# Values visits followed directly by scores, and transposes ahead of the first inputs, in a two-layer graph attention kernel

## The chip, the cores and the metric

The kernel runs on one core of one Trainium2 chip. The metric is the device time of one execution in microseconds, lower is better; the figure for a kernel is the median of its runs. All data are float32.

## The reference

The input is x with 64 graphs of 256 nodes and 512 features, and one adjacency matrix of 256 x 256 that all graphs share. Each of two layers normalises x, applies relu and adds its result to x. The first layer is masked attention of 8 heads with 64 features each, the second a graph attention with one score per node and side.

```python
    h = jnp.maximum(_layernorm(x, axis=-1), 0.0)
    x = x + _L0_gnn_ref(h, adj, L0_gnn_Wq, ..., L0_gnn_bo)
    h = jnp.maximum(_layernorm(x, axis=-1), 0.0)
    x = x + _L1_gnn_ref(h, L1_gnn_W, L1_gnn_a, L1_gnn_beta, adj)
# layer 0, of h: q, k, v = h @ Wq + bq, h @ Wk + bk, h @ Wv + bv, in heads
    scores = jnp.einsum('bqhd,bkhd->bhqk', q, k) / jnp.sqrt(jnp.float32(HD))
    scores = scores + (1.0 - adj)[None, None, :, :] * -1000000000.0
    attn = jax.nn.softmax(scores, axis=-1)
    out = jnp.einsum('bhqk,bkhd->bqhd', attn, v).reshape(b, n, d)
    return out @ Wo + bo
# layer 1, of h: h = h @ W, s1 = h @ a1, s2 = h @ a2
    e = jax.nn.leaky_relu(s1[:, :, None] + s2[:, None, :], negative_slope=ALPHA)
    e = e * mask[None, :, :]
    att = jax.nn.softmax(e, axis=2)
    h_prime = jnp.einsum('bij,bjf->bif', att, h)
    return jax.nn.elu(h_prime + beta * h)
```

## The kernel before

The graphs are worked on in 32 pairs. A pair's two graphs, with the two halves of their 512 features, form a matrix of 2 x 2 blocks, and every dense product (q and k, v, the output projection, the second layer's W) is computed in the Strassen manner with seven block products instead of eight. A `Unit` is one such product. `u.p(i)` issues product i: four matmuls on q's and k's side each (`UnitQK`, line 321) or eight matmuls (`UnitV`, `UnitO`, `UnitW`, line 354) of 128 x 128 by 256. Products are issued in the order 1, 4, 6, 2, 7, 5, 3. Products 2 and 3 add into the PSUM banks of products 1 and 5. `products` also calls what empties the banks: `put11` after product 2, `put2` after product 5, `put12` after product 3. So the bank of product 5, `b`, is written by PE, read by VectorE (DVE) in `put2` (lines 339, 455 or 562), added to by product 3, and read again in `put12`.

The sums of blocks that the seven products need are made by `combine_31`, `combine_2` and `combine_4`. For the output projection the two of `combine_31` are `o_blocks`, on GpSimd (POOL, line 427), and `combine_2` (line 273) on DVE subtracts from the second of them; product 6 of `UnitO` reads that.

Beside the dense products there are visits of the attention:

- `scores(b, q)`, line 385: for graph b and half q of the heads, 16 matmuls of 64-row tiles (two heads side by side in the array) into four banks; ScalarE (ACT, line 389) takes the exponential of each into a tile pt; POOL multiplies it by the mask (line 390) and adds its two halves into pp (line 392). A callback may be placed between these.
- `values(b, q)`: 32 matmuls of 32-column tiles (line 403) and 8 for the row sums (line 412); DVE takes the reciprocal (1.7 us), adds to acc and writes the tile oT (lines 414 to 417). It returns a closure that adds the reciprocals to acc on POOL (line 418); the closure is called at once or handed to the next scores as a callback.

The pt pool has four buffers, as many as one visit of scores fills, so each scores follows the values of the scores ahead of it. PSUM has eight banks, taken and given back in the order of the program.

For the second layer `gat_scores`, `gat_exp`, `divide` and `gat_t` make the attention matrix: DVE forms e (lines 488, 490), ACT takes the exponential, `divide` scales it on DVE (line 502), and PE transposes it (line 511, eight transposes for two graphs). `gat_z` multiplies (line 525), and `UnitW` ends the layer and stores.

The instruction order is written out by hand. `tc.manual_schedule` keeps each engine's instructions in the order of the program: for PE throughout, for DVE, ACT and POOL from `first` on. Only in most of `start` (all but the normalising and transposing of the first pair) a planner orders DVE, ACT and POOL by its own estimate. SyncE (SP) issues every DMA.

`start` handles pair 0's projections, `first` and `second` fill the pipeline, `round(p)` for p from 2 to 30 is the steady state, `last` and `end` drain it. One round runs the second layer of pair p - 2 (`UnitW`), the output projection of pair p - 1 (`UnitO`), the attention of pair p (graphs g0 and g1, four visits of scores and four of values) and the projections of pair p + 1 (`UnitQK` twice: ua and ub; `UnitV`: uv). In a round `x_t` transposes the next inputs on PE (line 300), `x_scales` and `y_scales` turn statistics into scales partly on POOL (lines 227 to 229), `y_normal` normalises on ACT (line 472), `y_sums` forms the node scores on DVE (line 478), and `residuals` loads x again and adds the bias on POOL (line 435).

Of the kernel before, what the change touches and what calls it, by code (L numbers as in the profile page):

```python
# [16 lines left out]
P = 128  # L17
# [6 lines left out]
def kernel(ctx: ExitStack, tc: tile.TileContext, x, adj, wq, bq, wk, bk, wv, bv, wo, bo, w, a, beta, out):  # L24
# [560 lines left out]
    def x_scales(p):  # L585
        SCALE["x", p] = scales(f"x{p}", 1)
# [8 lines left out]
    def y_stats_0(p):  # L595
        y_stats(p, 2 * NT, 0, 2 * p, 0)
# [5 lines left out]
    def y_stats_2(p):  # L602
        y_stats(p, 2 * NT, 0, 2 * p, 1)
# [25 lines left out]


    def start():
        with tc.manual_schedule(engines={ENG.DVE, ENG.Activation, ENG.Pool}):
            for g in range(2):
                for t in range(NT):
                    stats(f"x0{g}", NT, t, 0, XT[g, t])
                rstd, mr = scales(f"x0{g}", 1)
                nmr = minus(mr, f"x0{g}")
                for t in range(NT):
                    nc.scalar.activation(XT[g, t], XT[g, t], AF.Identity, bias=nmr[:, t:t + 1],
                                         scale=rstd[:, t:t + 1])  # L640
            x_t(0)
        combine_24(A["h", 0])
        load(1)
        ua, ub, uv = UnitQK(0, 0), UnitQK(0, 1), UnitV(0)
        products(ua, 1, 4, 6, 2, 7, 5)
        ub.p(1)
        products(ua, 3)
        products(ub, 4, 6, 2, 7, 5)
        masks()
        products(ub, 3)  # L650
        scores(0, 0)
        products(uv, 1, 4, 6, 2, 7, 5)
        wo_blocks = project_b()
        products(uv, 3)
        return wo_blocks

    def first():
        for i in range(2 * NT):
            x_stats(1, i)
        x_scales(1)  # L660
        add = values(0, 0)
        scores(0, 1, {1: add})
        x_normals(1, *range(2 * NT))
        x_t(1)
        load(2)
        s = A["h", 1]
        ua, ub, uv = UnitQK(1, 0), UnitQK(1, 1), UnitV(1)
        ua.p(1)
        combine_24(s)
        products(ua, 4, 6)  # L670
        prods = project_a()
        prods(0)
        products(ua, 2, 7)
        add = values(0, 1)
        prods(1)
        scores(1, 0, {1: add})
        products(ua, 5)
        ub.p(1)
        prods(2)
        products(ub, 4)  # L680
        products(ua, 3)
        products(ub, 6, 2)
        prods(3)
        add = values(1, 0)
        scores(1, 1, {1: add})
        products(ub, 7, 5)
        uv.p(1)
        products(ub, 3)
        prods(4)
        products(uv, 4)  # L690
        for i in range(2 * NT):
            x_stats(2, i)
        values(1, 1)()
        o_blocks(0)
        x_scales(2)
        products(uv, 6)
        combine_2(A["o", 0])
        products(uv, 2)
        x_normals(2, *range(2 * NT))
        products(uv, 7)  # L700
        combine_4(A["o", 0])
        products(uv, 5)
        residuals(0)
        prods(5)
        return uv

    def second(uv):
        p = 1
        scores(2, 0)
        products(uv, 3)  # L710
        uo = UnitO(0)
        products(uo, 1, 4, 6, 2)
        x_t(2)
        load(3)
        products(uo, 7)
        combine_2(A["h", 2])
        y_stats_0(0)
        products(uo, 5)
        add = values(2, 0)
        y_stats_1(0)  # L720
        combine_4(A["h", 2])
        ua, ub, uv = UnitQK(2, 0), UnitQK(2, 1), UnitV(2)
        products(uo, 3)
        y_stats_2(0)
        scores(2, 1, {1: lambda: (add(), y_scales(0))})
        ua.p(1)
        products(ua, 4)
        y_normal(0, 1)
        products(ua, 6, 2)
        y_normal(0, 0)  # L730
        products(ua, 7)
        y_sums(0, 1, 0, 1)
        add = values(2, 1)
        scores(3, 0, {1: add})
        products(ua, 5)
        ub.p(1)
        y_sums(0, 0, 0)
        products(ub, 4)
        products(ua, 3)
        products(ub, 6, 2)  # L740
        y_sums(0, 0, 1)
        add = values(3, 0)
        scores(3, 1, {1: add})
        gat_scores(1)
        gat_scores(0)
        products(ub, 7)
        gat_exp(1)
        gat_exp(0)
        products(ub, 5)
        uv.p(1)  # L750
        products(ub, 3)
        divide(0)
        products(uv, 4)
        gat_t(1)
        gat_t(0)
        values(3, 1)()
        products(uv, 6, 2)
        residuals(1)
        products(uv, 7, 5)
        gat_z(0)  # L760
        products(uv, 3)
        combine_24(A["z", 0])


    def round(p):
        g0, g1 = 2 * p, 2 * p + 1
        scores(g0, 0)
        uw = UnitW(p - 2)
        uw.p(1)
        x_stats(p + 1, 0)  # L770
        x_stats(p + 1, 1)
        uw.p(4)
        x_stats(p + 1, 2)
        x_stats(p + 1, 3)
        products(uw, 6, 2, 7, 5)
        uw.finish(0, 0, nc.gpsimd)
        x_scales(p + 1)
        o_blocks(p - 1)
        add = values(g0, 0)
        scores(g0, 1, {1: add})  # L780
        uw.p(3)
        combine_2(A["o", p - 1])
        x_normals(p + 1, 0, 1)
        uo = UnitO(p - 1)
        uo.p(1)
        uw.finish(1, 1, nc.vector)
        uw.put12()
        uw.finish(1, 0, nc.vector)
        x_normals(p + 1, 2, 3)
        uo.p(4)  # L790
        combine_4(A["o", p - 1])
        uo.p(6)
        uw.finish(0, 1, nc.vector)
        products(uo, 2)
        x_t(p + 1)
        if p + 2 < NP:
            load(p + 2)
        uo.p(7)
        combine_2(A["h", p + 1])
        y_stats_0(p - 1)  # L800
        products(uo, 5)
        add = values(g0, 1)
        y_stats_1(p - 1)
        combine_4(A["h", p + 1])
        products(uo, 3)
        y_stats_2(p - 1)
        scores(g1, 0, {1: lambda: (add(), y_scales(p - 1))})
        ua, ub = UnitQK(p + 1, 0), UnitQK(p + 1, 1)
        products(ua, 1, 4)
        y_normal(p - 1, 1)  # L810
        products(ua, 6)
        y_sums(p - 1, 1, 0, 1)
        products(ua, 2)
        y_normal(p - 1, 0)
        products(ua, 7, 5)
        y_sums(p - 1, 0, 0)
        add = values(g1, 0)
        scores(g1, 1, {1: add})
        products(ua, 3)
        y_sums(p - 1, 0, 1)  # L820
        products(ub, 1, 4, 6)
        gat_scores(g1 - 2)
        products(ub, 2)
        gat_exp(g1 - 2)
        gat_scores(g0 - 2)
        gat_exp(g0 - 2)
        products(ub, 7)
        divide(p - 1)
        products(ub, 5)
        values(g1, 1)()  # L830
        uv = UnitV(p + 1)
        uv.p(1)
        gat_t(g1 - 2)
        gat_t(g0 - 2)
        products(ub, 3)
        products(uv, 4, 6, 2)
        residuals(p)
        if p == NP - 2:
            o_blocks(p, "xt")
        products(uv, 7, 5)  # L840
        if p == NP - 2:
            combine_24(A["o", p])
        gat_z(p - 1)
        products(uv, 3)
        combine_24(A["z", p - 1])

    def last():
        p = NP - 1
        g0, g1 = 2 * p, 2 * p + 1
        scores(g0, 0)  # L850
        uo = UnitO(p - 1)
        products(uo, 1, 4, 6, 2)
        y_stats_0(p - 1)
        products(uo, 7, 5)
        add = values(g0, 0)
        y_stats_1(p - 1)
        products(uo, 3)
        y_stats_2(p - 1)
        scores(g0, 1, {0: lambda: y_scales(p - 1), 1: add})
        uw = UnitW(p - 2)  # L860
        products(uw, 1, 4)
        y_normal(p - 1, 1)
        products(uw, 6)
        y_sums(p - 1, 1, 0, 1)
        products(uw, 2)
        y_normal(p - 1, 0)
        products(uw, 7)
        add = values(g0, 1)
        y_sums(p - 1, 0, 0, 1)
        scores(g1, 0, {1: add})  # L870
        gat_scores(g1 - 2)
        gat_exp(g1 - 2)
        uw.p(5)
        gat_scores(g0 - 2)
        gat_exp(g0 - 2)
        uw.put2()
        uw.finish(0, 0, nc.gpsimd)
        divide(p - 1)
        uw.finish(1, 1, nc.vector)
        products(uw, 3)  # L880
        uw.finish(1, 0, nc.vector)
        add = values(g1, 0)
        scores(g1, 1, {1: add})
        uw.finish(0, 1, nc.vector)
        residuals(p)
        gat_t(g1 - 2)
        gat_t(g0 - 2)
        gat_z(p - 1)
        values(g1, 1)()
        o_blocks(p)  # L890
# [238 lines left out]
```

## Time and profile before

| what | us |
|---|---|
| median of 3 runs | 2918.84 |
| lowest and highest run | 2918.67, 2920.66 |
| the profiled execution | 2920.39 |
| its span from first to last instruction | 2918.5 |
| one steady round (start to start of one visit) | 88.77 |
| POOL pt<-pt,maskT, mean of one | 1.432 |
| POOL pp<-pt, mean of one | 0.827 |
| DVE reciprocal, mean of one | 1.743 |

The profiled execution took 1.9 us more than its span, and 1.6 us more than the median of the runs. In the profile, PE stands for TensorE's matmuls, PEld for its weight loads, which run beside them. A timeline line gives the start, the duration, the engine, the line, the operation with output and inputs, the tile shape, the count, and in brackets the idle time ahead of it with what ended it. The duration of a group of matmuls contains the way through the array, so the cost of a group is read from its start to the next group's start. TensorE's granted clock was 0.992 in the mean; it was full from 16.9 us on, but for short stretches near 68, 92 and in the last 110 us.

### The profile page before, as it was taken

How to read it: one execution, taken by the hardware profiler on the slowest of the kernel's cores; microseconds unless marked ns; L12 is line 12 of the kernel's file. 1: busy time of each engine (PE TensorE's matmuls, PEld its weight loads, DVE VectorE, ACT ScalarE, POOL GpSimd, SP SyncE). 2: the span in 40 equal slices, each digit the busy share in tenths (PEclk: the TensorE clock that was granted, in tenths of full speed). 3: DMA queues.
4: the chain of work that ended last, by engine and by line, in shares of the span. 5: the costliest groups of instructions: out<-in, count | busy, mean ns of one | idle time of the engine just before them, and what ended most of it. 6: DMA issues, size and time to landing. Idle time of an engine off the chain costs nothing.

```text
span 2918.5 us, 46465 instructions
## 1 busy us (share of the span) xinstructions
PE 2870.4 (98%) x18078; PEld 2340.9 (80%) x18078; DVE 2072.1 (71%) x3652; ACT 1043.2 (36%) x2116; POOL 1623.0 (56%) x1588
## 2 busy tenths in 40 slices
PE   8999999999999999999999999999999999999987
PEld 6778888888888888888888888888888888888865
DVE  5657866677767677766778676777666777667765
ACT  2233433333433333333334333334333333333332
POOL 2555655555655556655556555566555565555662
PEclk9999999999999999999999999999999999999998
DMA  5001111001111001110011110011110111100100
GB/s 149 25 11 34 44 44 44 19 26 44 44 44 44 15 30 44 44 44 28 24 37 44 44 44 15 30 44 44 44 43 13 32 44 44 44 23 22 30 30 30
DMA packets 96463, 110.00 MB, mean 38 GB/s; under 512 B 8560, under 2 KB 79472, under 8 KB 96240
## 3 DMA queue, kind: packets, MB, share of 16 engines
q1 hardware_dynamic: 96240, 106.99, 12.0%
q8 instruction: 145, 2.38, 0.3%
q14 instruction: 78, 0.64, 0.1%
HBM read 73.41 MB, written 33.55 MB: 37 GB/s over the span
## 4 chain that ended last, share of the span: by engine, by line
PE 93%; DVE 2%; POOL 2%; issue 2%; ACT 0%; DMA 0%; SPq 0%; POOLq 0%; DVEq 0%; ACTq 0%
PE qk_p L321 26%; PE o_p L354 13%; PE w_p L354 13%; PE v_p L354 13%; PE av L403 8%; PE sc L385 8%; PE pz L525 8%; PE sm L412 2%; PE tr L300 2%; PE at L511 1%; POOL pt L390 1%; POOL pp L392 1%; PE pe L154 0%; DVE pr L478 0%; DVE e L490 0%
## 5 line engine op out<-in xcount | busy, mean ns | idle before, releaser
L390 POOL TENSOR_TENSOR pt<-pt,maskT 128x512 f32<-128x512 f32 x512 | 733.3, 1432 | 772.8 <-ACT pt L389 772.8
L392 POOL TENSOR_TENSOR pp<-pt 128x256 f32<-128x256 f32 x512 | 423.4, 827 | 39.8
L389 ACT ACTIVATE pt<-sc 128x512 f32<-128x512 f32 x512 | 264.4, 603 | 427.4 <-PE sc L385 427.3
L478 DVE SCALAR_TENSOR_TENSOR pr<-h,war 128x512 f32<-128x512 f32 x256 | 298.9, 1211 | 59.2 <-ACT h L472 59.2
L385 PE MATMUL sc<-qk 64*128 64x256 f32 x2048 | 256.4, 390 | 0.0
L403 PE MATMUL av<-pt,v 128*32 128x256 f32 x4096 | 252.4, 383 | 3.0 <-POOL pt L390 3.0
L418 POOL TENSOR_TENSOR acc<-acc,rec 128x256 f32<-128x256 f32 x128 | 109.7, 857 | 253.5 <-DVE acc L415 250.3
L385 PEld LDWEIGHTS sc<-qk 64*128 64x128 f32 x2048 | 187.8, 187 | 65.0 <-issue 20.6
L414 DVE RECIPROCAL rec<-sm 128x256 f32<-128x256 f32 x128 | 223.0, 1743 | 13.9 <-PE sm L412 13.9
L525 PE MATMUL pz<-eT,h 128*128 128x256 f32 x1024 | 229.2, 383 | 3.1 <-ACT eT L512 3.1
L525 PEld LDWEIGHTS pz<-eT,h 128*128 128x128 f32 x1024 | 196.5, 192 | 30.6 <-ACT eT L512 3.6
L403 PEld LDWEIGHTS av<-pt,v 128*32 128x32 f32 x4096 | 130.8, 110 | 105.1 <-issue 40.6
L321 PE MATMUL qk_p<-s_h,wq_t 128*128 128x256 f32 x768 | 198.5, 381 | 0.9 <-DVE s_h L273 0.9
L321 PE MATMUL qk_p<-s_h,wk_t 128*128 128x256 f32 x768 | 197.4, 380 | 0.0
L354 PE MATMUL o_p<-wo_t,s_o 128*128 128x256 f32 x768 | 178.5, 382 | 0.0
L354 PE MATMUL w_p<-w_t,s_z 128*128 128x256 f32 x768 | 177.5, 381 | 0.0
L354 PE MATMUL v_p<-wv_t,s_h 128*128 128x256 f32 x768 | 176.4, 379 | 0.0
L532 DVE TENSOR_TENSOR s_z<-pz,z 128x512 f32<-128x512 f32 x64 | 44.3, 691 | 182.2 <-ACT z L528 182.2
L528 ACT COPY z<-pz 128x512 f32<-128x512 f32 x128 | 74.9, 585 | 254.3 <-PE pz L525 254.3
L354 PEld LDWEIGHTS o_p<-wo_t,s_o 128*128 128x128 f32 x768 | 141.3, 190 | 27.2 <-issue 10.5
L321 PEld LDWEIGHTS qk_p<-s_h,wk_t 128*128 128x128 f32 x768 | 146.4, 191 | 19.9
L354 PEld LDWEIGHTS w_p<-w_t,s_z 128*128 128x128 f32 x768 | 146.4, 191 | 19.8
(165 smaller groups left out, 5681.4 us busy)
## 6 DMA issues: line engine op xcount, KB each, us to landing
x<-in_x_dram SPq DMA_DIRECT2D x128, 256.0 KB, 3.7
y<-in_x_dram SPq DMA_DIRECT2D x128, 256.0 KB, 2.9
out_dram<-o SPq DMA_DIRECT2D x128, 256.0 KB, 2.2
wq_b<-in_L_gnn_Wq_dram SPq DMA_DIRECT2D x4, 256.0 KB, 5.4
wk_b<-in_L_gnn_Wk_dram SPq DMA_DIRECT2D x4, 256.0 KB, 5.9
wv_b<-in_L_gnn_Wv_dram SPq DMA_DIRECT2D x4, 256.0 KB, 5.0
wo_b<-in_L_gnn_Wo_dram SPq DMA_DIRECT2D x16, 64.0 KB, 2.1
w_b<-in_L_gnn_W_dram SPq DMA_DIRECT2D x4, 256.0 KB, 3.3
```

Of the source, the lines that this page charges most:

```text
L321: nc.tensor.matmul(ps[:, j * N:(j + 1) * N], wj[i][:, c, ft * P:(ft + 1) * P], s[i][:, c, :], start=(start and j == 0 and c == 0), stop=(c ...
L354: nc.tensor.matmul(ps[:, t * N:(t + 1) * N], s[i][:, c, t * P:(t + 1) * P], wj[i][:, c, :], start=(start and t == 0 and c == 0), stop=(c = ...
L385: nc.tensor.matmul(pss[2 * pair + h][:, k * N:(k + 1) * N], qk[hs, 1, k * P:(k + 1) * P], qk[hs, 0, :], start=True, stop=True)
L389: nc.scalar.activation(pt, two(pss[i]), AF.Exp, scale=QSCALE)
L390: nc.gpsimd.tensor_tensor(pt, pt, maskT, ALU.mult)
L392: nc.gpsimd.tensor_tensor(pp, pt[:, 0, :], pt[:, 1, :], ALU.add)
L403: nc.tensor.matmul(ps[i * HH:(i + 1) * HH, s * N:(s + 1) * N], v[:, k, c0:c0 + HH], pts[i][:, k, :], start=(k == 0), stop=(k == NT - 1))
L414: nc.vector.reciprocal(rec, sums[:, :N])
L418: return lambda: nc.gpsimd.tensor_tensor(acc, acc, rec, ALU.add)
L478: nc.vector.scalar_tensor_tensor(pr, H2[g][:, t, :], 1.0, war[:, j, :], op0=ALU.mult, op1=ALU.mult, accum_out=SC[g][:, t, j:j + 1])
L525: nc.tensor.matmul(ps[:, f * N:(f + 1) * N], h2[:, k, fs], eT[:, k, :], start=(k == 0), stop=(k == NT - 1))
L528: nc.scalar.copy(dst, two(ps))
```

## The change

There are two parts. In `start`, 36 transposes of the identity into a bank of its own are put at the head of PE's order, ahead of the first pair's transposes. In `first`, `second` and `round`, the order is changed so that values and scores stand side by side:

- The first scores of the next pair, `scores(g0, 0)`, move from the head of a round (or of `second`, `last`) into the round ahead, directly behind that round's last values. These values move behind ub's product 3 and uv's product 4. The POOL addition to acc, called at once before, becomes a callback of the scores. `residuals` comes behind the scores.
- The output projection's products 7, 5 and 3 are all issued ahead of `values(g0, 1)`, so that `scores(g1, 0)` follows these values directly; `x_t` and the next load stand between products 5 and 3.
- `y_stats_0` follows product 7, `y_stats_2` follows `y_stats_1`, and in a round `o_blocks` comes ahead of `x_scales`.

```diff
     def start():
+        warm = bank("warm")
+        for i in range(36):
+            nc.tensor.transpose(warm[:, i % 4 * P:(i % 4 + 1) * P], ident, ident)
         with tc.manual_schedule(engines={ENG.DVE, ENG.Activation, ENG.Pool}):
...
         products(uv, 4)
         for i in range(2 * NT):
             x_stats(2, i)
-        values(1, 1)()
+        add = values(1, 1)
         o_blocks(0)
         x_scales(2)
+        scores(2, 0, {1: add})
         products(uv, 6)
...
     def second(uv):
-        p = 1
-        scores(2, 0)
         products(uv, 3)
         uo = UnitO(0)
-        products(uo, 1, 4, 6, 2)
+        products(uo, 1, 4, 6, 2, 7)
+        y_stats_0(0)
+        products(uo, 5)
         x_t(2)
         load(3)
-        products(uo, 7)
+        products(uo, 3)
         combine_2(A["h", 2])
-        y_stats_0(0)
-        products(uo, 5)
         add = values(2, 0)
         y_stats_1(0)
+        y_stats_2(0)
         combine_4(A["h", 2])
         ua, ub, uv = UnitQK(2, 0), UnitQK(2, 1), UnitV(2)
-        products(uo, 3)
-        y_stats_2(0)
         scores(2, 1, {1: lambda: (add(), y_scales(0))})
...
         gat_t(1)
         gat_t(0)
-        values(3, 1)()
+        add = values(3, 1)
+        scores(4, 0, {1: add})
+        residuals(1)
         products(uv, 6, 2)
-        residuals(1)
         products(uv, 7, 5)
...
     def round(p):
         g0, g1 = 2 * p, 2 * p + 1
-        scores(g0, 0)
         uw = UnitW(p - 2)
...
         uw.finish(0, 0, nc.gpsimd)
+        o_blocks(p - 1)
         x_scales(p + 1)
-        o_blocks(p - 1)
         add = values(g0, 0)
...
-        products(uo, 2)
+        products(uo, 2, 7)
+        y_stats_0(p - 1)
+        products(uo, 5)
         x_t(p + 1)
         if p + 2 < NP:
             load(p + 2)
-        uo.p(7)
+        products(uo, 3)
         combine_2(A["h", p + 1])
-        y_stats_0(p - 1)
-        products(uo, 5)
         add = values(g0, 1)
         y_stats_1(p - 1)
+        y_stats_2(p - 1)
         combine_4(A["h", p + 1])
-        products(uo, 3)
-        y_stats_2(p - 1)
         scores(g1, 0, {1: lambda: (add(), y_scales(p - 1))})
...
         divide(p - 1)
         products(ub, 5)
-        values(g1, 1)()
         uv = UnitV(p + 1)
         uv.p(1)
         gat_t(g1 - 2)
         gat_t(g0 - 2)
         products(ub, 3)
-        products(uv, 4, 6, 2)
+        uv.p(4)
+        add = values(g1, 1)
+        scores(g1 + 1, 0, {1: add})
         residuals(p)
+        products(uv, 6, 2)
         if p == NP - 2:
             o_blocks(p, "xt")
...
     def last():
         p = NP - 1
         g0, g1 = 2 * p, 2 * p + 1
-        scores(g0, 0)
         uo = UnitO(p - 1)
```

## The prediction

> **What bounds the kernel now.** I read the page first, for the share of each engine and the chain that ended last.
>
> ```profile
> PE 2870.4 (98%) x18078; PEld 2340.9 (80%) x18078; DVE 2072.1 (71%) x3652; ACT 1043.2 (36%) x2116; POOL 1623.0 (56%) x1588
> ...
> PE 93%; DVE 2%; POOL 2%; issue 2%; ACT 0%; DMA 0%; SPq 0%; POOLq 0%; DVEq 0%; ACTq 0%
> ```
>
> TensorE (PE) is the bound: 98% busy, 93% of the chain. A change counts only if it takes time out of PE's own order or makes PE wait. From 100 to 2800 us the waits view names 1.0 us of PE waiting: the steady rounds, 88.77 us each, have almost no bubbles left, and almost none of the slack that covers them is visible. So next I read the PE timeline of one round, for the starts of groups.
>
> ```profile
> 1403.11 1.03 PE L321 MATMUL qk_p<-s_h,wk_t 128*128 128x256 f32 x4
> 1404.07 1.99 PE L403 MATMUL av<-pt,v 128*32 128x256 f32 x32
> 1405.82 0.67 PE L412 MATMUL sm<-pp,ones 128*32 128x256 f32 x8
> 1406.42 2.00 PE L385 MATMUL sc<-qk 64*128 64x256 f32 x16
> 1408.35 1.13 PE L321 MATMUL qk_p<-s_h,wq_b 128*128 128x256 f32 x4
> 1409.32 1.03 PE L321 MATMUL qk_p<-s_h,wk_b 128*128 128x256 f32 x4
> ...
> 1420.12 1.03 PE L321 MATMUL qk_p<-s_h,wk_t 128*128 128x256 f32 x4
> 1421.08 1.93 PE L403 MATMUL av<-pt,v 128*32 128x256 f32 x32
> 1422.83 0.61 PE L412 MATMUL sm<-pp,ones 128*32 128x256 f32 x8
> 1423.37 1.99 PE L354 MATMUL v_p<-wv_b,h 128*128 128x256 f32 x8
> 1425.20 1.04 PE L511 MATMUL at<-ident,e 128*128 128x128 f32 x8
> 1426.08 1.03 PE L321 MATMUL qk_p<-s_h,wq_b 128*128 128x256 f32 x4
> ...
> 1465.43 1.89 PE L354 MATMUL o_p<-wo_t,oT 128*128 128x256 f32 x8
> 1467.32 1.97 PE L354 MATMUL o_p<-wo_t,s_o 128*128 128x256 f32 x8
> 1469.12 1.89 PE L354 MATMUL o_p<-wo_b,oT 128*128 128x256 f32 x8
> ```
>
> A full-array product of 4 takes 0.865 us start to start, one of 8 takes 1.73. The first block is a values visit directly followed by scores; the second is values alone. In the third, product 6 of UnitO starts 0.16 us late. Then the DVE timeline beside the second block, since the change takes away the values visit that stands there.
>
> ```profile
> 1422.59 0.88 DVE L502 SCALAR_TENSOR_TENSOR e<-e,grec,betai 128x256 f32<-128x256 f32 x2
> 1423.39 0.48 DVE L339 SCALAR_TENSOR_TENSOR qk<-qk_p,bq,qk_u 128x256 f32<-128x256 f32 x1
> 1423.78 0.48 DVE L339 SCALAR_TENSOR_TENSOR qk<-qk_p,bk,qk_u 128x256 f32<-128x256 f32 x1
> ```
>
> DVE runs without a pause from 1401.79 to 1428.0, so it is behind PE here: it empties ub's fifth product, which PE finished at 1421.1, only at 1424.26.
>
> **What the Trainium skill says.** "TensorEngine Tiling (Array Packing)", Key Properties: changing the tiling mode drains TensorE. The trace agrees: each step between full tiles, 128*32 and 64*128 costs 0.02 to 0.2 us. "TensorE: Matmul & The Clock Gate", Part 1: cold PE runs at half clock until a 3413 ns window was busy. It agrees: four products take 1.71 us before 16 us, 0.86 after. "SBUF — State Buffer", Who interferes with whom: a DVE instruction with two SBUF inputs and a GpSimd instruction that reads SBUF exclude each other. It agrees: combine_2 takes 1.74 us beside a POOL pt operation, 0.69 alone.
>
> **The change part by part.**
>
> *Merged visits.* Values alone: 1420.12 to 1425.20 is 5.08, less 0.865 + 1.73 + 0.43 + 1.73 of work, leaves 0.33 us. Scores alone in the same round: v_p starts 1443.35, scores 1445.17, w_p 1447.09, its next 1448.92: 5.57 less 3 x 1.73 leaves 0.38. Together 0.71. Merged, first block: 1403.11 to 1409.32 is 6.21 less 5.62, 0.59; the other merged visit of the round (1454.10 to 1463.71, 9.61 less 9.08) has 0.53. So a merge saves 0.12 to 0.18, I take 0.15. Merges: 2 in each of 29 rounds, 1 in first, 2 in second, 61 in all: **-9.2 us** (-7 to -11).
>
> *o_blocks ahead of x_scales.* UnitO's product 6 waits for combine_2 (DVE, ends 1467.17), which waits for the second of two POOL operations that queue behind x_scales' POOL part and end at 1465.40. POOL is idle from 1457.03 to 1461.37, so in front of x_scales the two (2.51 us) end near 1459.6. combine_2 then follows the oT operation (ends 1463.8) and ends, a collision on the shared port included, by 1464.8, where PE wants it at 1467.1. Gone are 0.16 of wait and 0.07 of refill (1467.32 to 1469.12 is 1.80): 0.23 x 29 = **-6.7 us**. x_scales' POOL part stays at its time, since it waits for DVE's bn_aggr (1460.91).
>
> *The cover that is gone.* The new PE order after ub's product 5 is V's product 1, eight transposes, ub's product 3. Values (2.3 us) no longer stand ahead. V's product 1 can start at 1420.99, the transposes at 1422.72, product 3 at 1423.60. The transposes' last e half ends at 1423.47 (0.3 us late for the second of e's two). Product 3 adds into the bank that the two L339 read, until 1424.26. The cost of just this wait is seen at the start: there product 3 begins at 39.46 where L339 ended at 39.40, and its first 4 take 0.97 instead of 0.865. So product 3 starts at 1424.32: 0.72 + 0.10 = 0.82 us a round, x 29 = **+23.8 us**. Behind product 3 in PE's queue stand V's product 4, values and scores; they and all their readers come later by the same, and nothing makes it up, since PE has no idle time to give. Does DVE get there sooner? Its unbroken run starts with the h of y_normal, which waits for y_scales on POOL (rstd at 1487.59, after the acc add that ends at 1487.50; bn_aggr was done at 1487.39), and this add stands 7.1 us behind the start of scores(g1,0) through four POOL operations, in both orders. I followed DVE's new order from product 6 of UnitO: combine_2 done 2 us sooner, put12 after product 3 (about 1479.4), reciprocal at 1480.15, six bn_stats, combine_4, bn_aggr near 1486.2; POOL reaches its turn at 1487.1, 7.1 behind the new start of scores (1479.98). POOL decides, so DVE keeps its distance to PE. Bounds: one port collision is worth 0.45 us (POOL pt 1.72 instead of 1.27); one fewer leaves 0.37, one more 1.27 a round: +11 to +37.
>
> *Start.* 36 transposes at some 0.21 us cold fit ahead of x's, which are ready at 7.67. But the built order differs elsewhere: ACT now has mask's exponential ahead of the four relu, and DVE has one wv_t ahead of s_h.
>
> ```profile
> 15.54 0.63 ACT L143 ACTIVATE mask<-mask 128x512 f32<-128x512 f32 x1 [2.03 <-DVE mask L142]
> ```
>
> The exponential can't run before 15.54, so the relu begin at 16.1 (before: at 10.97, the same view) and PE's first product at 16.75 instead of 12.67, perhaps cold again after 4 us of idleness. Product 6 needs combine_2 behind DVE's reordered queue: 16.55 (wv landed), wv_t, s_h, three wv_t, s_h, bn_stats, 0.6 to 0.65 each, so near 21.45; before it started at 19.23. Loss 2.3 to 2.7, **+2.5 us**. Even a warm clock could gain nothing here: product 6 already waited for DVE.
>
> *Moved at no cost.* x_t comes 3.46 us later: four relu (2.03) fit into the 5.8 us to qk's product 1, L306 and combine_2 end some 4.3 us on, wanted after 9. Its 4 x loads on SP issue later by the same, for a reader 63 us on (3.7 to landing). residuals' four POOL adds (4.95) go behind the 8.2 us of pt and pp; their y is read a third of a round later, and SP's four y loads have no new wait. V's product 6 takes the first scores bank: released 1.22 + 0.58 after scores start, wanted at 1.93; at worst 0.1 x 29 = 3 us. combine of z: needed two products after pz, 5.2 us, done in 3.2. In round 30 o_blocks queues behind all this, up to 1 us once.
>
> *Sum.* -9.2 - 6.7 + 23.8 + 2.5 = +10.4. Against the profiled 2920.39 (span 2918.5 plus 1.9 around it) 2930.8; the median of the runs stands 1.55 lower, so **2929**.
>
> **The rivals.**
> *No stall, faster.* DVE frees ub's bank before PE wants it. Against it: DVE's unbroken run. For it: combine_2 and the put operations end sooner. It decides if the second L339 ends 0.72 us sooner, by 1423.54. Then -9.2 - 6.7 + 2.5 = -13.4: 2905.
> *Balance.* One collision fewer, stall and refill 0.37: -2.7, 2916; two thirds of the stall, +2.5, 2921.
> *More stall.* bn_aggr comes after POOL's turn (margin 0.9), or V's product 6 waits: each 0.5 us a round adds 14.5 us, 2944.
> *The warming doesn't do what it says*: it is in every case, +2.5, with 0 and +4 as ends.
>
> **How the numbers follow.** 0.2% (5.8 us) is about what a measurement here can tell from no change. Main case with more stall: 0.7, its own range 2925 to 2944; balance 0.22; no stall 0.08. The balance case spans about 2914 to 2924; the range takes most of it: 2916 to 2942. Slower 0.70, same 0.21, faster 0.09.
>
> **What would show it.** Right: about 29 waits of at L511 on DVE e (0.3 us) and of qk_p on DVE L339 (0.45); UnitO's product 6 on time; scores right after sm everywhere; first qk_p near 16.7 behind mask. Wrong: none of these waits in the rounds, or a first qk_p at 12.

## The result, and the profile after

| | before | after |
|---|---|---|
| median, 12 runs each, us | 2918.61 | 2925.18 |
| lowest and highest, us | 2914.83, 2920.66 | 2923.64, 2927.59 |
| profiled execution, its span, us | 2920.39, 2918.5 | 2925.39, 2923.6 |
| one steady round, mean (lowest), us | 88.779 (88.747) | 88.916 (88.900) |
| scores(0,0) starts, us | 41.38 | 45.38 |
| first w_p product of the first steady round, us | 204.06 | 205.64 |

The ratio is 1.0024, with a 95% interval of 1.0015 to 1.0033: slower, by a quarter of a per cent, and clear of the noise. The forecast was 2929, from 2916 to 2942. Runs of several of these kernels fall into two groups some 4 us apart, the faster at the higher granted clock; e2_warm_only below, for one, is 3.1 us slower than the kernel before in either group, while its median is 2.7 slower.

The profiled executions differ by 5.0 us. The start loses 4.0, the filling of the pipeline gives 2.4 back (45.38 to 205.64 is 160.26; before, 162.68), the 28 intervals between rounds lose 28 x 0.137 = 3.8, and the end gains 0.4. What was given back is taken up with the start, further below.

The page of the changed kernel, the same two parts as for the one before: busy time by engine, and the chain that ended last.

```profile
PE 2869.9 (98%) x18114; PEld 2338.8 (80%) x18114; DVE 2062.6 (71%) x3652; ACT 1049.8 (36%) x2116; POOL 1616.2 (55%) x1588
...
PE 39%; DVE 25%; POOL 20%; issue 12%; ACT 3%; DMA 0%; POOLq 0%; SPq 0%; DVEq 0%; ACTq 0%
```

PE's busy time has hardly moved, though there are 36 more matmuls. The chain tells the difference: it was 93% PE, now it leaves PE in every round and goes through DVE and POOL. A wait that costs under 1% of a round is enough to redirect it, so the shares say where the chain runs and not what the detour costs.

The waits view from 100 to 2800 us has a row that the kernel before did not have (total us, times, longest us):

```profile
PE qk_p L321 <- DVE qk L339: 6.9, 29, 0.2
```

The PE timeline of one round, at the place of the second block shown of before, and at UnitO:

```profile
1425.37 1.36 PE L511 MATMUL at<-ident,e 128*128 128x128 f32 x8
1426.96 1.13 PE L321 MATMUL qk_p<-s_h,wq_b 128*128 128x256 f32 x4 [0.24 <-DVE qk L339]
1427.93 1.03 PE L321 MATMUL qk_p<-s_h,wk_b 128*128 128x256 f32 x4
...
1430.61 1.93 PE L403 MATMUL av<-pt,v 128*32 128x256 f32 x32
1432.37 0.61 PE L412 MATMUL sm<-pp,ones 128*32 128x256 f32 x8
1432.91 2.00 PE L385 MATMUL sc<-qk 64*128 64x256 f32 x16
...
1468.72 1.89 PE L354 MATMUL o_p<-wo_t,oT 128*128 128x256 f32 x8
1470.44 1.89 PE L354 MATMUL o_p<-wo_t,s_o 128*128 128x256 f32 x8
1472.17 1.89 PE L354 MATMUL o_p<-wo_b,oT 128*128 128x256 f32 x8
```

The eight transposes and ub's product 3 now follow V's product 1 at once. Start to start, the transposes take 1.59 us where eight need 0.87: 0.32 of it lies inside the group (its last matmul starts at 1426.45 instead of 1426.13), because e is late, above all its second half, and 0.40 stands between the group and product 3, of which the waits view names 0.24. Product 3's first four take 0.97 instead of 0.865; such extra time of the first group behind a wait is called refill in this document. That is 0.72 + 0.10 = 0.82 us a round. Scores follow the values directly, and UnitO's product 6 (o_p<-wo_t,s_o) is on time: 1.72 and 1.73 between the last starts, where 1.89 and 1.80 stood before.

DVE beside it:

```profile
1425.24 0.88 DVE L502 SCALAR_TENSOR_TENSOR e<-e,grec,betai 128x256 f32<-128x256 f32 x2
1426.04 0.48 DVE L339 SCALAR_TENSOR_TENSOR qk<-qk_p,bq,qk_u 128x256 f32<-128x256 f32 x1
1426.43 0.48 DVE L339 SCALAR_TENSOR_TENSOR qk<-qk_p,bk,qk_u 128x256 f32<-128x256 f32 x1
```

The second L339 ends at 1426.91, and product 3, which adds into the bank that it reads, starts at 1426.96.

The start, on PE, of the kernel before:

```profile
12.67 1.91 PE L321 MATMUL qk_p<-h,wq_b 128*128 128x256 f32 x4
...
19.23 1.13 PE L321 MATMUL qk_p<-s_h,wq_t 128*128 128x256 f32 x4 [0.87 <-DVE s_h L273]
```

and of the changed kernel, with ACT below it:

```profile
1.46 5.97 PE L634 MATMUL warm<-ident 128*128 128x128 f32 x36 [1.46 <-POOL ident masks.py:199]
...
17.33 2.08 PE L321 MATMUL qk_p<-h,wq_b 128*128 128x256 f32 x4 [4.17 <-ACT h L302]
19.20 1.91 PE L321 MATMUL qk_p<-h,wk_b 128*128 128x256 f32 x4
20.90 1.72 PE L321 MATMUL qk_p<-h,wq_t 128*128 128x256 f32 x4
...
23.32 1.03 PE L321 MATMUL qk_p<-s_h,wq_t 128*128 128x256 f32 x4
...
16.16 0.63 ACT L143 ACTIVATE mask<-mask 128x512 f32<-128x512 f32 x1 [4.52 <-DVE mask L142]
16.70 2.04 ACT L302 ACTIVATE h<-tr 128x512 f32<-128x512 f32 x4
```

The relu (h, L302) stand behind the mask's exponential on ACT, so the first product waits until 17.33. By then the clock is down again ("cold", half of full speed; "warm" is full speed): three groups of four take 1.87, 1.70 and 1.56 us where a warm one takes 0.86. The record of the granted clock has half speed from 12.06 to 22.30 us. It fell just behind PE's wait for the second graph's x (1.70 us idle ahead of 10.99), and the wait for the relu followed before it rose again. In the traces of e3 and e8 below, with the same start, it fell at 14.90 and 15.37, inside the wait for the relu.

### The profile page after: what moved, and what is told of

Read it like the earlier page. It is cut to its first block, busy times and chain, and to the rows that moved or that the text cites. A ratio compares the mean times of both kernels' runs of the same rounds, so it can differ in the third digit from the quotient of the medians.

```text
span 2923.6 us, 46397 instructions
## 1 busy us (share of the span) xinstructions
PE 2869.9 (98%) x18114; PEld 2338.8 (80%) x18114; DVE 2062.6 (71%) x3652; ACT 1049.8 (36%) x2116; POOL 1616.2 (55%) x1588
## 4 chain that ended last, share of the span: by engine, by line
PE 39%; DVE 25%; POOL 20%; issue 12%; ACT 3%; DMA 0%; POOLq 0%; SPq 0%; DVEq 0%; ACTq 0%
PE v_p L354 11%; PE w_p L354 11%; POOL pt L390 9%; DVE pr L478 9%; PE pz L525 8%; POOL pp L392 6%; PE qk_p L321 4%; DVE qk L339 3%; PE av L403 2%; PE sc L385 2%; POOL acc L418 2%; DVE e L490 2%; DVE e L502 2%; DVE rec L414 2%; DVE e L488 2%
## 5 line engine op out<-in xcount | busy, mean ns | idle before, releaser
L390 POOL TENSOR_TENSOR pt<-pt,maskT 128x512 f32<-128x512 f32 x512 | 718.1, 1403 | 808.4 <-ACT pt L389 808.4
L392 POOL TENSOR_TENSOR pp<-pt 128x256 f32<-128x256 f32 x512 | 432.6, 845 | 39.8
L554 POOL TENSOR_TENSOR o<-o,m 128x512 f32<-128x512 f32 x36 | 45.9, 1277 | 337.2 <-ACT m L546 302.0
L403 PEld LDWEIGHTS av<-pt,v 128*32 128x32 f32 x4096 | 120.5, 110 | 113.4 <-issue 32.3
L354 PEld LDWEIGHTS v_p<-wv_t,s_h 128*128 128x128 f32 x768 | 143.4, 190 | 28.5 <-ACT pt L389 10.3
```

Source lines behind the costliest of these rows:

```text
L354: nc.tensor.matmul(ps[:, t * N:(t + 1) * N], s[i][:, c, t * P:(t + 1) * P], wj[i][:, c, :], start=(start and t == 0 and c == 0), stop=(c = ...
L390: nc.gpsimd.tensor_tensor(pt, pt, maskT, ALU.mult)
L392: nc.gpsimd.tensor_tensor(pp, pt[:, 0, :], pt[:, 1, :], ALU.add)
L403: nc.tensor.matmul(ps[i * HH:(i + 1) * HH, s * N:(s + 1) * N], v[:, k, c0:c0 + HH], pts[i][:, k, :], start=(k == 0), stop=(k == NT - 1))
```

## The experiments

All times below are against the kernel before on the same chip; "round" is the mean length of a steady round in the profile. Each ratio has its 95% interval in brackets.

### The start apart from the rounds

**e1_order_only**: the changed kernel without the 36 transposes.

```diff
     def start():
-        warm = bank("warm")
-        for i in range(36):
-            nc.tensor.transpose(warm[:, i % 4 * P:(i % 4 + 1) * P], ident, ident)
```

> The changed order without the 36 transposes at the start. My theory (the start costs about 4 us at its first scores, of which the stalls of the pipeline's filling give 2.4 back; each steady round is 0.15 us longer): first qk_p near 12.7, about 3.5 to 4.5 us slower than before, rounds of 88.91 us. Rival (the start is the whole loss, the round's lengthening is an artefact of a shifted profile): no slower than before, rounds of 88.77.

Measured: 2922.09 against 2918.26, 1.0019 [1.0011, 1.0027]; rounds of 88.918; first qk_p at 12.01, scores(0,0) at 41.47.

**e2_warm_only**: the kernel before, with these three lines and nothing else of the change.

> The kernel before with the 36 transposes at the start and nothing else. My theory: ACT's mask exponential comes ahead of the relu, first qk_p near 17, first scores 4 us late, 1.5 to 4 us slower at the end, rounds unchanged at 88.77. Rival (the transposes are harmless and the delay comes with the new order): first qk_p at 12.7 or earlier, no change or 1 to 2 us faster.

Measured: 2920.95, 1.0008 [1.0000, 1.0017]; rounds of 88.777; first qk_p at 16.95, scores(0,0) at 44.98. What the two lose, 3.8 and 2.7, adds up to 6.5 beside the change's 6.6, so the start and the rounds look independent of each other, though each of these differences has an interval of over 2 us to either side. That the rounds lose is plain. e2's interval reaches down to no change; that its start loses rests on the late first product as well, and on e1, which is 3.1 below the changed kernel (2925.18 - 2922.09).

### The stall in the rounds

**e3_cover**: the changed kernel with one line moved.

```diff
         uv.p(1)
+        uv.p(4)
         gat_t(g1 - 2)
         gat_t(g0 - 2)
         products(ub, 3)
-        uv.p(4)
```

> The changed kernel with V's product 4 ahead of the eight transposes, so that PE asks for ub's bank 1.73 us later than in the changed kernel. My theory (PE stalls 0.84 us a round on the e and the L339 of a DVE that is behind): the stall goes, rounds 0.84 shorter (88.07), 29 rounds, 24 us faster than the changed kernel, about 2901. Rival (DVE is the bound of the round, so the wait turns up at another place, at V's product 6 or at the first scores bank): the rounds stay within 0.2 of 88.91 and the time near 2925.

Measured: 2901.08, 0.9945 [0.9932, 0.9959], rounds of 88.090. PE's timeline of the same place:

```profile
1415.80 1.04 PE L511 MATMUL at<-ident,e 128*128 128x128 f32 x8
1416.67 1.03 PE L321 MATMUL qk_p<-s_h,wq_b 128*128 128x256 f32 x4
1417.54 1.03 PE L321 MATMUL qk_p<-s_h,wk_b 128*128 128x256 f32 x4
```

The transposes take their 0.87 and product 3 has neither a wait nor a refill. 1.73 us of V's product 4 ahead of the readers take away 88.916 - 88.090 = 0.826 us a round, against 0.82 of stall and refill. All of the loss in the rounds is this one missing cover: with it they are shorter than those of before.

**e8_half_cover**: the same line, put between the two gat_t and ub's product 3.

```diff
         uv.p(1)
-        uv.p(4)
         gat_t(g1 - 2)
         gat_t(g0 - 2)
+        uv.p(4)
         products(ub, 3)
```

> The changed kernel with V's product 4 between the two gat_t and ub's product 3 (in e3_cover it stands ahead of the gat_t too). My theory: the stall is two waits, the eight transposes 0.32 us for e's second half, and ub's product 3 0.40 for the second L339 with 0.10 of refill. V's product 4 (1.73) covers the second and not the first: rounds of 88.09 + 0.32 = 88.41 or, with a refill, 88.51; 2910 to 2914. Rival: the wait on e is part of PE's run-ahead and costs nothing by itself: rounds of 88.09, 2901.

Measured: 2911.18, 0.9975 [0.9967, 0.9983], rounds of 88.419.

```profile
1420.39 1.35 PE L511 MATMUL at<-ident,e 128*128 128x128 f32 x8
1421.58 1.89 PE L354 MATMUL v_p<-wv_t,h 128*128 128x256 f32 x8
1423.31 1.03 PE L321 MATMUL qk_p<-s_h,wq_b 128*128 128x256 f32 x4
```

From the start of the transposes to the next group it is 1.19 us: the 0.32 for e is still there (88.419 - 88.090 = 0.329), and the wait of product 3 is gone with its refill. The stall is two waits, and the one inside the transposes, which the waits view does not name, is 40% of it.

### The gains, one by one

**e4_oblocks**: the kernel before, with o_blocks ahead of x_scales and nothing else.

```diff
-        x_scales(p + 1)
         o_blocks(p - 1)
+        x_scales(p + 1)
```

> The kernel before with o_blocks ahead of x_scales in a round and nothing else. My theory: UnitO's product 6 no longer waits for combine_2, 0.23 us a round, 29 rounds, 6.7 us faster than before (2912), rounds of 88.53. Rival (combine_2 then collides with POOL's pt operation on the shared port and ends no sooner): no change.

Measured: 2909.5, 0.9974 [0.9964, 0.9985], rounds of 88.485. Less than the usual round of before, 88.764, by 0.28. Of it 0.23 is UnitO's product 6 with its refill. The other 0.05 is in the values that stand ahead of scores(g1,1): there PE waited a little for a pt of POOL, so that from the row sums (sm) to the scores it took 0.60 us, and now takes 0.55. The likely reason is that POOL is rid of two operations earlier.

**e5_merge_uo**: the kernel before, with UnitO's reordering alone.

```diff
-        products(uo, 2)
+        products(uo, 2, 7)
+        y_stats_0(p - 1)
+        products(uo, 5)
         x_t(p + 1)
...
-        uo.p(7)
+        products(uo, 3)
         combine_2(A["h", p + 1])
-        y_stats_0(p - 1)
-        products(uo, 5)
         add = values(g0, 1)
         y_stats_1(p - 1)
+        y_stats_2(p - 1)
         combine_4(A["h", p + 1])
-        products(uo, 3)
-        y_stats_2(p - 1)
```

> The kernel before with one edit: in every round UnitO's products 7, 5 and 3 and x_t move ahead of values(g0,1), so that this visit is directly followed by scores(g1,0); all else is as before. 29 merges, no other move. The prediction priced a merge at 0.15 us: -4.4 us, rounds of 88.63. What the trace of the changed kernel suggests instead is 0.20 (entry into the second tiled visit 0.095, first full group after it 0.10): -5.8 us, rounds of 88.58. Rival: the gain of the changed order comes from the o_blocks move and from the merge at the round's end alone, and this merge gives its gain back to x_t and combine_2 coming 3.5 us later: 0, rounds of 88.78.

Measured: 2922.35, 1.0017 [1.0009, 1.0025], rounds of 88.951. Neither expectation holds: the merge alone makes the round 0.17 to 0.19 us longer. Its PE timeline around UnitO's product 3:

```profile
1476.74 1.91 PE L300 MATMUL tr<-ident,x 128*128 128x128 f32 x16
1478.63 1.99 PE L354 MATMUL o_p<-wo_b,s_o 128*128 128x256 f32 x8
1480.56 1.93 PE L403 MATMUL av<-pt,v 128*32 128x256 f32 x32
```

The sixteen transposes need 1.74, but product 3 starts after 1.89 and takes 1.93 instead of 1.83 to the next group: 0.15 of wait and 0.10 of refill. Before, the values (1476.14 to 1478.43, 2.29 us) lay between product 5 and product 3; now the transposes do, with 1.74. DVE's sum over product 5's bank ends at 1478.58, just ahead of product 3:

```profile
1477.90 0.68 DVE L455 TENSOR_TENSOR o_p<-o_p,o_u 128x512 f32<-128x512 f32 x1
```

It is late because DVE's whole run through UnitO begins with combine_2, which waits 1.64 us for POOL. In the values ahead of scores(g1,1) the wait for POOL's pt grows from 0.05 to 0.18. So -0.20 + 0.15 + 0.10 + 0.13 = +0.18.

**e10_uo_oblocks**: both edits together.

> The kernel before with two edits, o_blocks ahead of x_scales (e4_oblocks, rounds 0.28 shorter) and UnitO's products 7, 5 and 3 ahead of values(g0,1), so that it is followed by scores(g1,0) (e5_merge_uo, rounds 0.17 longer). Theory: the merge alone lost since combine_2, late behind POOL, made DVE's sums of UnitO late for product 3, and POOL's second pt late for av; with o_blocks ahead DVE and POOL are early enough and the merge gives its 0.197: rounds of 88.485 - 0.197 = 88.29, 0.476 x 29 = -13.8 us, 2904.5. Rival: the effects add: -0.28 + 0.17, rounds of 88.66, 2915.

Measured: 2904.79 against 2918.81, 0.9953 [0.9939, 0.9967], rounds of 88.287. Now the merge gives 88.485 - 88.287 = 0.198, and in the trace product 3 has neither wait nor refill (1.82 us to the next group). The two edits do not add: the one is +0.17 alone and -0.20 behind the other, because o_blocks' move gives DVE and POOL the lead that the merge uses up.

**e11_end_merge**: the changed order in first, second and at a round's end with e3_cover's cover, without warming, and with the other two edits of the round undone.

```diff
+        uv.p(4)
         gat_t(g1 - 2)
         gat_t(g0 - 2)
         products(ub, 3)
-        uv.p(4)
...
+        x_scales(p + 1)
         o_blocks(p - 1)
-        x_scales(p + 1)
```

(UnitO's lines are the ones of the kernel before again.)

> The kernel e6_cover_no_warm with the other two edits of the rounds undone: x_scales ahead of o_blocks again and UnitO's order with values(g0,1) alone again. What is left in a round is the merge of values(g1,1) with the next round's scores(g0,0), V's product 4 as the cover ahead of ub's product 3, and residuals behind the scores; first and second keep the changed order. If this merge gives its 0.197 by itself: rounds of 88.57, -5.7 us and up to 0.6 from the three merges of first and second: 2912 to 2913. Rival: as with UnitO's merge, the moved work comes late without o_blocks' move, and the rounds stay at 88.7 or more: 2916 or above.

Measured: 2911.73, 0.9978 [0.9970, 0.9986], rounds of 88.598 in the mean, most near 88.59. With its cover this merge gives 0.18 by itself (88.779 - 88.598). With the other two edits in place it gives 88.287 - 88.090 = 0.197, e10 against e6 below.

### What warming does at the start

**e7_warm_act**: the kernel before with the 36 transposes, and with all of start after x_t(0) in the program's order on ACT.

```diff
+        with tc.manual_schedule(engines={ENG.Activation}):
             combine_24(A["h", 0])
             load(1)
...
```

> The kernel before plus the 36 transposes, with ACT's order alone held to that of the program over the whole start, so that the mask's exponential comes after the relu and after ub's evictions; DVE's and POOL's orders stay as in e2_warm_only. If the exponential ahead of the relu is what costs, the first qk_p starts near 12.1 instead of 16.95, and product 6 still waits for combine_2 behind wv's loads and sums on DVE: 19.3 to 21, so +0 to +1.7 us against the kernel before, and no gain from a warm clock. If warming itself is of use once ACT is in order, the first eight products save some 1.7 us of half-clock time and product 6 comes before 19.2: -1 us or more. If neither (the transposes themselves delay the start), it stays at +2.7.

Measured: 2919.3 against 2918.31, 1.0009 [1.0000, 1.0017]; first qk_p at 12.26, scores(0,0) at 46.59.

```profile
12.26 1.03 PE L321 MATMUL qk_p<-h,wq_b 128*128 128x256 f32 x4
...
21.73 2.08 PE L321 MATMUL qk_p<-s_h,wq_t 128*128 128x256 f32 x4 [4.92 <-DVE s_h L273]
23.60 1.91 PE L321 MATMUL qk_p<-s_h,wk_t 128*128 128x256 f32 x4
```

With ACT in order the first products run at 12.26 and warm. Then product 6 waits 4.92 us for DVE, whose order is still the changed one, and PE is cold again behind that wait. The four groups from 21.73 take 6.26 us where e2_warm_only, warm there, takes 3.45; so scores(0,0) comes 1.6 us behind e2_warm_only, though product 6 came 1.2 us sooner than there. The time fits the first of the three expectations, but product 6 came later than it said (21.73, not 19.3 to 21). So ACT's order alone was not the cause of the late product 6: DVE's was enough to bring it 2.5 us later than in the kernel before. In the whole time, an interval that begins at no change leaves open what this costs.

**e9_warm28**: 28 transposes in place of 36, which leaves the built order of ACT and DVE as in the kernel before.

```diff
+        warm = bank("warm")
+        for i in range(28):
+            nc.tensor.transpose(warm[:, i % 4 * P:(i % 4 + 1) * P], ident, ident)
```

> The kernel before plus 28 identity transposes in place of 36. With this many, the built order of ACT and DVE over the whole start is that of the kernel before: the mask's exponential after the relu, combine_2 ahead of the last sum of wv. If what cost 2.7 us in e2_warm_only is the reordering alone, the first qk_p starts near 12.1 on a warm clock, the first products take 0.87 each instead of 1.71, and product 6 waits for DVE's combine_2 as before, at 19.2: 0 against the kernel before, within 0.5 us. Rival 1: the warm clock is worth its 1.7 to 2.5 us: 2916. Rival 2: the products that now end sooner leave PE idle for over 3 us before product 6, and it runs cold from there: +1 to +2.5 us.

Measured: 2917.74 against 2918.81, 0.9999 [0.9991, 1.0007].

```profile
11.81 1.03 PE L321 MATMUL qk_p<-h,wq_b 128*128 128x256 f32 x4
...
19.26 1.57 PE L321 MATMUL qk_p<-s_h,wq_t 128*128 128x256 f32 x4 [2.81 <-DVE s_h L273]
20.63 1.91 PE L321 MATMUL qk_p<-s_h,wk_t 128*128 128x256 f32 x4
```

The loss is gone with the reordering, and no gain takes its place. The first groups are 0.86 us instead of 1.71, product 6 starts at 19.26 where it was 19.23 before, and the idle 2.81 us ahead of it bring the clock down again, so that scores(0,0) is 1.7 us later than before. The second rival was right that PE would be cold there. By the first w_p product (203.26 against 204.06) that has been made up: this trace lacks a cold stretch near 92 us that the kernel before has, of which more below.

### The version that beats both

**e6_cover_no_warm**: e3_cover without the transposes.

> The changed kernel with V's product 4 ahead of the two gat_t and ub's product 3 (as in e3_cover), and without the 36 identity transposes. If the start and the rounds are independent, it lies below e3_cover (2901.1) by what e2_warm_only lost (2.7) or by what e1_order_only saved (3.1): 2898 to 2898.5, ratio 0.9932 to the kernel before, with the first qk_p near 12.0 and rounds of 88.09. Rival: the fill between 60 and 200 us absorbs the start's delay, so that the warm-up costs nothing by the end: 2901.

Measured: 2897.37 against 2918.31, 0.9938 [0.9924, 0.9952]; rounds of 88.090, first qk_p at 12.23. It is 3.7 us below e3_cover (3.8 with each against its own runs of before), near the 3.1 by which e1_order_only is below the changed kernel (2.7 in the same way).

## Why the prediction was right, step by step

| step | predicted, us | measured, us | from |
|---|---|---|---|
| merged visits | -9.2 (0.15 each) | -12 (0.198 and 0.197 in a round, taken for all 61) | e10 against e4, e6 against e10 |
| o_blocks ahead of x_scales | -6.7 (0.23 a round) | -8.1 (0.28 a round) | e4 |
| cover gone | +23.8 (0.82 a round) | +24.0 (0.826 a round) | after against e3 |
| start | +2.5 | +1.6 in this pair of traces; +3.1 in medians | first w_p product; after against e1 |
| sum | +10.4 | +5.5; +7.0 | |

The two sums go with the 5.0 us between the profiled executions and the 6.6 between the medians.

**The cover** was right in place, mechanism and size: the second half of e, the second L339 and the refill, 0.82. e8 shows the split. DVE, and not PE, sets this point. By the traces POOL's turn keeps DVE where it is, so that DVE's earlier work in UnitO did not shorten the stall: the add to acc ends 7.0 us behind the start of scores(g1,0) in the changed kernel (1490.23 and 1483.21), where it was 7.1 before, and bn_aggr was done at 1489.30, 0.9 ahead of it. No run moved POOL's turn, so this part is read and not tried. Of the signs named, the 29 waits at L339 are in the waits view; those at L511 are not, and show only from start to start.

**The merges** were sized too small. I took a merged visit of before as the price, and the first of the two had a wait of 0.05 in it, for POOL's pt, that is no part of a visit. Its 0.12 pulled the mean to 0.15; the other end, 0.18, was nearer.

**o_blocks** was right for product 6 (0.16 and 0.07). The 0.05 that the same move takes out of the wait for POOL's pt was not in the sum.

**"Moved at no cost"** held in the changed kernel, but the list did not say that part of it leans on another part. e5 shows UnitO's product 3 late for L455 when o_blocks stays where it was. The prediction priced the parts as if each stood alone, and the sum came out because all were made together. It used the lead ("combine_2 done 2 us sooner") for the stall, but did not name it as a condition of the merge; that part was luck.

**The start** was right in the cause and too low in size, 2.5 against 3.1. Product 6 came at 23.32 and not 21.45. Its sum s_h was ready at 22.57: wv's first sum began 0.54 later than assumed (17.09, not 16.55), and DVE idled 0.50 for the late relu. The other 0.75 is the clock: products 1 and 4 ahead of it ran mostly cold, which the text had as "perhaps" and left out of the sum. One reading was wrong and did no harm: 36 transposes at 0.21 us, begun at 1.46, would end at 9.0 and not ahead of x's at 7.67. They took 5.97 us, since the clock rose at 5.24.

So scores(0,0) lost 4.0 in these traces. Then 2.4 came back, at two places. Near 70 us the shift between the two traces falls from 4.0 to 3.3, near 92 from 3.2 to 1.6. At both, the traces have PE waits and cold stretches. In the windows view (busy us and count of PE, PEld, DVE, ACT, POOL, then the granted clock) of the kernel before, in the stretch behind a 1.98 us wait of ub's product 3 that ends at 90.73:

```profile
90.00:95.00 5.00, 4.27 (x13) 3.52 (x14) 4.33 (x14) 0.00 (x0) 2.48 (x3) 0.70 0.16 52
```

and of the changed kernel, behind the same wait of 1.98 us that ends at 93.97:

```profile
95.00:100.00 5.00, 5.00 (x33) 3.97 (x35) 4.64 (x19) 0.54 (x2) 0.79 (x1) 1.00 0.08 28
```

The same idle time is followed by a cold stretch of 3.41 us in the one and not in the other. The clock records of the 13 traces tell them apart. In each, the granted clock changes only on a grid with steps of 3.41 us, and this wait is in all of them, 1.97 to 1.98 us long. In the eight traces where the cold stretch follows (before, e4, e5, e6, e7, e8, e10, e11) the wait lies within one step, beginning 0.21 to 1.32 us into it. In the five without (after, e1, e2, e3, e9) it begins 1.43 us or more into a step and ends at the next step or beyond. So where the wait falls on the grid goes with the cold stretch in every trace, though no run set it on purpose. "TensorE: Matmul & The Clock Gate" of the Trainium skill, Part 1, says that the window which decides on the clock runs freely, so that the number of cold matmuls differs from run to run. The traces agree in that. They do not agree that a cold clock takes a whole idle window of 3.4 us: 1.98 us were enough here.

The gain is therefore no part of the change. After, e3 and e8 have the same code up to the first w_p product and reach it at 205.64, 205.10 and 207.14 us. Only e8 has the cold stretch near 92, as the kernel before has, and against that (204.06) it is 3.1 late, as much as the medians of after and e1 differ.

**"A warm clock could gain nothing"** was right, and e9 shows it: product 6 waits for DVE in either case, and the time is that of before. That the wait would even make the gain cold again was not foreseen.

**The rivals.** No stall is refuted by the 29 waits, and e3 shows that it would have come with one line moved: 2901 then, 2905 in the forecast. Balance (0.37 a round) and more stall are refuted by 0.82. The forecast of +10.4 is 3.8 above the 6.6 between the medians: the merges gave 2.8 more than priced and o_blocks 1.4 more, and the start, priced 0.6 too low, took a little of that back.

## What to carry to other kernels

When an edit takes work away that stood between a producer's eviction and its next reader, the gain of the edit is one number and the cover is another: look up on the evicting engine when the bank comes free, and put a product that needs nothing from it in the gap. Price parts of a change together with what they lean on, since the same merge was worth +0.17 or -0.20 us a round according to whether another engine had been given a lead. And look at what warming a clock sets off: in none of these runs did it pay, since a wait behind the warm work brought the clock down again (e7, e9), and 36 added instructions made the planner of the other engines choose another order.

## What the runs showed of the hardware that was not expected

- Identity transposes alone bring PE to full clock: in e9's trace they take 0.213 us each from 1.73 to 6.19 us, and 0.109 from there.
- The granted clock changes only on a grid of 3.41 us, and the same wait of 1.98 us was followed by 3.41 us of half clock in the eight traces where it lies within one step of the grid, and by none in the five where it does not. At the start it was the same with longer waits: 2.81 us within a step (e9) were followed by half-clock products, 2.45 us across a step (e1) by full-speed ones.
- A visit to the 128*32 and 64*128 tiles costs 0.095 us on entry and 0.10 in the first full group after it. At full clock the first group after a wait of PE took 0.07 to 0.10 more as well, whether 0.15 or 2 us were waited.
- The waits view counts from the end of the last matmul, which lies about 0.16 us behind the start of the next one in a group without waits. So it named 0.24 of the 0.40 us ahead of product 3, and nothing of the 0.32 inside the transposes.
